# A mixture of experts behind two attentions on one core: blocks of tokens fetched in four parts and transposed in squares of 32 on VectorE

## The chip, the cores and the metric

The kernel runs on one core of a Trainium2 chip. The metric is device time in microseconds for one execution; the kernel before takes 810.36 us (median of 3 runs, 809.91 to 810.59). A core has five engines that matter here: TensorE (PE; its weight loads are listed as PEld), VectorE (DVE), ScalarE (ACT), GpSimd (POOL), and SyncE (SP), which in this kernel only issues DMAs. Each engine works off its own queue in order.

## The reference

2048 tokens (64 sequences of 32) of 256 values pass through cross-attention, self-attention and a mixture of 8 experts, each behind a normalization or on the sum so far. All is in float32. The change touches the experts:

```python
h_NM2H = jnp.einsum('md,ndh->nmh', x_MD, Wl1) + bl1[:, None, :]
a_NMH, b_NMH = (h_NM2H[..., :H], h_NM2H[..., H:])
y_NMD = jnp.einsum('nmh,nhd->nmd', jax.nn.silu(a_NMH) * b_NMH, Wl2) + bl2[:, None, :]
y_MD = jnp.einsum('mn,nmd->md', ew_MN, y_NMD)
```

Here D = 256 and H = 512. `ew_MN` holds the two largest router weights of each token, divided by their sum, and zeros elsewhere. The sum over `d` in the first line is what needs the tokens with their 256 values laid along the partitions.

## The kernel before, in words

**Tokens.** Sixteen tiles of 128 tokens go through cross-attention (64 sequences, `seqs`), self-attention (`self_attention`, L382) and the router (`route`, L470). For each token the router writes a row of `RW` = 265 values (256 normalized values, 8 expert weights, the token's number) to two places of a table in DRAM, `routed`, which has a region of 2048 rows for each expert. These writes are indirect DMAs of POOL (L521), two for each tile of tokens.

**Blocks.** The experts' work is cut into blocks of 128 table rows that belong to one expert. Six "early" blocks are started while the last tokens are still on their way, and 28 "late" blocks follow (up to 33 are provided for; those from 28 on stand in an `If` that isn't entered with these data). A table of where each block begins and whose it is (`meta`) is formed on DVE, for the late blocks in `late_blocks` (L732 to L801), when the last tokens have been counted.

A block takes these steps of the class `Blocks`:

- `gathered` (L608): SP reads the block's first row from `meta` (a TENSOR_LOAD, L586) and issues one DMA of 128 rows x 1060 bytes into the tile xg, one token to a partition. There are five xg buffers.
- `weights` (L614): SP loads the expert's first matrix with its biases (wall1, "W1", 1028 KB) and the second (wall2, "W2", 640 KB) into one of three lanes. A register condition leaves a load out where the lane already holds this expert.
- `prepared` (L624): PE transposes the two halves of xg into a PSUM bank (L629), and ACT copies them to xT (L631), which has two buffers. DVE takes from xg the block's gates and the row numbers to which the results go (L634 to L640).
- `first_half` and `second_half` (L645, L662): PE multiplies xT by the expert's first matrix, eight matmuls each (L657): pa for the gated half, pb for the other. Each shows as two records in the trace. ACT applies silu to pa (L671), DVE multiplies with pb (L676) to g.
- `combined` (L683): PE multiplies g by the second matrix (L688), DVE adds the bias and multiplies by the gate (L693, L694), and POOL adds y to the output by an indirect DMA (L695).

**What sets the order.** The order on SP and PE is the program's (`manual_schedule`, L79); the other engines' order is the planner's, which may bring an instruction forward when its inputs are there. The steps around the last tokens are written out by hand in `do(...)` (L1042 to L1067): x is `prepared`, a and b the halves, c `combined`. The five gathers of the first early blocks are issued at L1017, the sixth at L1058. When `late_blocks` has been called, SP gets the gathers of late blocks 0 to 2 (L1063), then the weights of late block 1 (L1066); late block 0 works with expert 0, whose weights were loaded long before (L1038). Then `run` (L1073) interleaves: in step b it gathers block b + 3, prepares block b + 1, does the first half of b, combines b - 1, loads W2 for b + 2, does the second half of b and loads W1 for b + 3. In the first step `last_early` (L1103) combines the last early block and loads the weights of late block 2.

Of the kernel before, what the change touches and what calls it, by code (L numbers as in the profile page):

```python
# [9 lines left out]
FP = mybir.dt.float32  # L10
U32 = mybir.dt.uint32
AF = mybir.ActivationFunctionType
ALU = mybir.AluOpType
# [3 lines left out]
P = 128  # L17
D = 256
TOK = 2048
NT = TOK // P  # L20
SEQ = 32
# [8 lines left out]
NE = 8  # L30
HID = 512
CAP = TOK
RW = D + NE + 1
# [17 lines left out]
def block_kernel(  # L51
# [23 lines left out]
    nc = tc.nc  # L75
# [4 lines left out]
    const = ctx.enter_context(tc.tile_pool(name="const", bufs=1))  # L80
# [3 lines left out]
    ident = const.tile([P, P], FP, name="ident")  # L84
# [22 lines left out]
    def pool(name, bufs):  # L107
        return ctx.enter_context(tc.tile_pool(name=name, bufs=bufs))
# [19 lines left out]
    for i in range(4):  # L128
        w = slice(4 * HD * i, 4 * HD * (i + 1))
# [29 lines left out]
    routed = tc.dram_tile([NE * CAP, RW], FP, name="routed")  # L159
# [5 lines left out]
    xp = pool("xp", 3)  # L165
    tb = pool("tb", 1)

    def bank(shape, name):
        return ps.tile([P] + shape, FP, tag="a", name=name)
# [415 lines left out]
    def number(meta, k, b, most):  # L585
        return nc.values_load(  # L586
            meta[0:1, k, b : b + 1],
            engines=[SP],
            min_val=0,
            max_val=most,  # L590
            skip_runtime_bounds_check_because="formed from counts that bound it",
        )

    class Blocks:
# [11 lines left out]
            self.xgs, self.xTs, self.ps, self.gs, self.experts = {}, {}, {}, {}, {}  # L606

        def gathered(self, b):  # L608
            xg = xp.tile([P, RW], FP, tag="xg", bufs=5, name=f"xg_{self.name}{b}")
            at = number(self.meta, 0, b, NE * CAP - P)  # L610
            nc.sync.dma_start(out=xg, in_=routed[bass.ds(at, P), :])
            self.xgs[b] = xg

        def weights(self, b, layers, sure=False):  # L614
            if b not in self.experts:
# [7 lines left out]

        def prepared(self, b):  # L624

            xg = self.xgs.pop(b)
            pt = bank([2, P], f"pxT_{self.name}{b}")
            for k in range(2):
                nc.tensor.transpose(pt[:, k, :], xg[:, k * P : (k + 1) * P], ident)  # L629
            xT = xp.tile([P, 2, P], FP, tag="bxT", bufs=2, name=f"bxT_{self.name}{b}")  # L630
            nc.scalar.copy(xT, pt)  # L631
            self.xTs[b] = xT
            gates = xp.tile([P, NE], FP, tag="gates", name=f"gates_{self.name}{b}")
            nc.vector.tensor_tensor(gates, xg[:, D : D + NE], self.mine[:, b, :], ALU.mult)  # L634
            one = slice(b, b + 1)
            nc.vector.tensor_reduce(self.gate[:, one], gates, AX.X, ALU.add)
            if self.valid is None:
                nc.vector.tensor_copy(self.to[:, one], xg[:, RW - 1 : RW])
            else:
                nc.vector.scalar_tensor_tensor(  # L640
                    self.to[:, one], xg[:, RW - 1 : RW], self.valid[:, one],
                    self.spare[:, one], ALU.mult, ALU.add,
                )

# [7 lines left out]
        def of_half(self, b, half):  # L652
            w, _ = lanes[self.lane(b)]
            for j in range(4):
                for k in range(2):
                    lo = k * 2 * HID + (half * 4 + j) * P
                    nc.tensor.matmul(  # L657
                        self.ps[b][half][:, j, :], w[:, lo : lo + P], self.xTs[b][:, k, :],
                        start=(k == 0), stop=(k == 1),
                    )  # L660

# [275 lines left out]

    seen = const.tile([P, NE], FP, name="seen")
    nc.gpsimd.memset(seen, 0.0)
    none = xp.tile([P, RW], FP, tag="xg", bufs=5, name="none")  # L940
    nc.gpsimd.memset(none, 0.0)

    for e in range(NE):
# [231 lines left out]
```

## Time and profile before

| what | value |
|---|---|
| median of 3 runs | 810.36 us |
| the profiled execution's own time | 811.05 us |
| its span, first to last instruction | 809.3 us |
| PE busy | 778.6 us (96%) |
| DVE busy | 496.9 us (61%) |
| ACT busy | 378.3 us (47%) |
| first early gather is issued | 579.34 us |
| first late gather is issued | 638.97 us |
| last late block's last y is added by POOL from | 800.53 us |

Times of instructions are counted from the span's start. In a timeline, each line has the start, the duration, the engine, the line of the kernel, the operation, what is written and read, and how many instructions were merged; brackets hold the idle time of the engine before it and what ended it. "SPq" is SP's queue: the time is that of the issue, not of the transfer. A matmul's duration includes the way through the array, so successive ones overlap, and what a group costs is read from the starts of its neighbours. In a view of windows the columns are the window, its length, the busy time of PE, PEld, DVE, ACT and POOL, the granted clock of PE (1.00 is full), the mean busy share of the 16 DMA engines, and GB/s.

The trace also holds a record for each DMA packet with its start, size and duration. In the late blocks, a gather's packets are 1060 bytes long, those of W1 8224 and those of W2 5120.

### The profile page before, as it was taken

The page shows a single profiled execution, that of the slowest core. Times are in us where ns is not written, and L with a number is a line of the kernel's source. Part 1 is how long each engine was busy: PE and PEld are TensorE (multiplying, and loading weights), DVE is VectorE, ACT ScalarE, POOL GpSimd, SP SyncE. Part 2 cuts the span into 40 slices and gives each one's busy share as a digit, 9 for nine tenths or more (in the row PEclk, how much of TensorE's full clock was granted, in tenths as well). Part 3 has the DMA queues.
Part 4 walks back from the last instruction along what each step waited for, and adds up shares of the span by engine and source line. Part 5 has one row for each costly group of instructions (what it writes and reads, how often), then busy time and mean ns, then how long its engine had stood idle before and what let it go on. Part 6 is the DMA issues. An engine that isn't in the chain of part 4 may idle for free. (4 is left out here: it accounts for less than half of the span.)

```text
span 809.3 us, 15134 instructions
## 1 busy us (share of the span) xinstructions
PE 778.6 (96%) x5212; PEld 612.5 (76%) x5212; DVE 496.9 (61%) x2045; ACT 378.3 (47%) x1078; POOL 143.7 (18%) x195
## 2 busy tenths in 40 slices
PE   8899999999999999999999999999998999999994
PEld 7576777677767767777767777676677899999994
DVE  4657666766686677677677766768665734334332
ACT  3564555556465555556554555555435322222220
POOL 3001011120201011111101110121123313333332
PEclk9999999999999999999999999999999999999998
DMA  9440202021020202022020102020441495356321
GB/s 306 140 112 1 66 11 67 11 89 51 27 79 11 67 10 80 10 75 65 27 66 11 66 11 67 14 73 15 163 162 34 114 398 144 54 139 210 60 41 21
DMA packets 32735, 64.14 MB, mean 79 GB/s; under 512 B 5328, under 2 KB 23632, under 8 KB 31120
## 3 DMA queue, kind: packets, MB, share of 16 engines
q1 hardware_dynamic: 26128, 54.08, 19.8%
q0 software_dynamic: 6528, 9.06, 6.2%
q8 instruction: 43, 0.70, 0.4%
q14 instruction: 36, 0.29, 0.1%
HBM read 87.54 MB, written 13.16 MB: 124 GB/s over the span
## 5 line engine op out<-in xcount | busy, mean ns | idle before, releaser
L314 ACT ACTIVATE pr<-s,nmx 128x257 f32<-128x257 f32 x256 | 121.7, 479 | 110.1 <-DVE nmx L313 101.9
L313 DVE TENSOR_REDUCE nmx<-s 128x1 f32<-128x257 f32 x256 | 105.8, 421 | 70.3 <-PE s L309 69.7
L309 PE MATMUL s<-kv,q 128*128 128x257 f32 x512 | 142.8, 387 | 1.6 <-ACT pr L314 1.4
L342 PE MATMUL pa<-pt,kv 128*128 128x512 f32 x256 | 123.3, 604 | 5.3 <-ACT ov L366 5.3
L309 PEld LDWEIGHTS s<-kv,q 128*128 128x128 f32 x512 | 89.1, 192 | 16.1 <-ACT pt L336 3.0
L332 PEld LDWEIGHTS tp<-ident,pr 128*128 128x128 f32 x512 | 61.5, 144 | 30.4 <-issue 15.7
L321 DVE TENSOR_SCALAR pr<-pr,inv 128x256 f32<-128x256 f32 x256 | 82.3, 363 | 3.3
L521 POOL DMA_INDIRECT routed<-xr,rslots x32 | 32.9, 1027 | 283.6 <-DVE lastT L1006 215.9
L332 PE MATMUL tp<-ident,pr 128*128 128x128 f32 x512 | 80.2, 278 | 1.6 <-DVE pr L321 1.6
L345 ACT COPY cT<-pa 128x512 f32<-128x512 f32 x64 | 37.5, 585 | 89.3 <-PE pa L342 89.3
L336 ACT COPY pt<-tp 128x512 f32<-128x512 f32 x128 | 75.4, 590 | 6.3 <-PE tp L332 6.0
L342 PEld LDWEIGHTS pa<-pt,kv 128*128 128x128 f32 x256 | 46.1, 190 | 39.8 <-issue 28.3
L695 POOL DMA_INDIRECT out_x<-y_late,to_late x28 | 43.5, 1555 | 107.3 <-DMA out_x<-y_late,to_late 33.5
L285 PE MATMUL pqh<-xqT,xwq_sb 128*128 128x256 f32 x256 | 60.8, 381 | 0.8 <-ACT xqT L192 0.8
L375 PE MATMUL po<-xwo_sb,ov 128*128 128x256 f32 x256 | 60.3, 379 | 0.0
L375 PEld LDWEIGHTS po<-xwo_sb,ov 128*128 128x128 f32 x256 | 48.6, 190 | 6.6
L285 PEld LDWEIGHTS pqh<-xqT,xwq_sb 128*128 128x128 f32 x256 | 47.4, 190 | 7.9 <-ACT xqT L192 1.5
L314 ACT ACTIVATION_READ_ACCUMULATOR pr<-s,nmx 128x1 f32 x256 | 51.7, 202 | 0.0
L319 DVE RECIPROCAL inv<-sums 128x2 f32<-128x2 f32 x128 | 20.5, 160 | 44.3 <-ACT pr L314 44.0
L631 ACT COPY bxT_late<-pxT_late 128x256 f32<-128x256 f32 x28 | 10.4, 372 | 73.1 <-PE pxT_late L629 73.1
L390 PE MATMUL pqkv<-awqkv_sb,xaT 128*128 128x512 f32 (+1 forms) x128 | 43.9, 486 | 0.0
L350 POOL TENSOR_TENSOR xb<-x,xbo_bc 128x256 f32<-128x256 f32 x16 | 11.6, 726 | 165.8 <-issue 117.2
(259 smaller groups left out, 1284.0 us busy)
## 6 DMA issues: line engine op xcount, KB each, us to landing
lane<-in_wall SPq DMA_DIRECT2D x24, 1028.0 KB
lane<-in_wall SPq DMA_DIRECT2D x24, 640.0 KB
lane2a<-in_wall SPq DMA_DIRECT2D x10, 1028.0 KB
kv<-in_ctx_t SPq DMA_DIRECT2D x16, 514.0 KB
kv<-in_ctx_a SPq DMA_DIRECT2D x16, 512.0 KB
lane2b<-in_wall SPq DMA_DIRECT2D x10, 640.0 KB
xg_late<-routed SPq DMA_DIRECT2D x28, 132.5 KB
x<-in_x SPq DMA_DIRECT2D x16, 128.0 KB
```

The lines of the kernel that those rows point to most:

```text
L285: nc.tensor.matmul(pq[:, mm, :], xwq_sb[:, k, m * P : (m + 1) * P], xqT[:, k, :], start=(k == 0), stop=(k == 1),)
L309: nc.tensor.matmul(s, qb[:, g * P : (g + 1) * P], kvT[:, b, :], start=True, stop=True)
L313: nc.vector.tensor_reduce(nmx, s, AX.X, ALU.max, negate=True)
L314: nc.scalar.activation(pr[:, g, :], s, AF.Exp, bias=nmx, accum_out=sums[:, g : g + 1])
L321: nc.vector.tensor_scalar(pr[:, i, :ML], pr[:, i, :ML], inv[:, i : i + 1], None, ALU.mult)
L332: nc.tensor.transpose(tp[:, g * P : (g + 1) * P], pr[:, g, j * P : (j + 1) * P], ident)
L336: nc.scalar.copy(pt, tp)
L342: nc.tensor.matmul(pa, kvA[:, b, j, :], pts[j], start=(j == 0), stop=(j == MC - 1))
L345: nc.scalar.copy(cT[:, :, b, :], pa.rearrange("p (h n) -> p h n", n=SEQ))
L375: nc.tensor.matmul(po, ov[:, m, :], xwo_sb[:, m, :], start=False, stop=(m == XH // 2 - 1))
L390: nc.tensor.matmul(pq, xaT[:, k, :], awqkv_sb[:, k, lo:hi], start=(k == 0), stop=(k == 1))
L695: nc.gpsimd.indirect_dma_start(out=out[:, :], out_offset=bass.IndirectOffsetOnAxis(ap=self.to[:, b : b + 1], axis=0), in_=y, in_offset=Non ...
```

## The change

The block's rows are fetched in five DMAs. Four of them bring 64 of the 256 values each, to a quarter of the partitions: partition 32a + i of xg then holds values 64a to 64a + 63 of tokens i, 32 + i, 64 + i and 96 + i. The fifth brings the last nine values of each row (weights and number) to a new tile xw, one token to a partition. One DVE instruction transposes all squares of 32 x 32 of xg into xT, so that partition 32a + i of xT holds values 64a + i and 64a + 32 + i of the 128 tokens. The two PE transposes, the PSUM bank and the ACT copy go. Since this orders the 256 values differently over the partitions, the rows of the first matrix are laid out in the same order on the host. The matmul of L657 then reads its moving operand as four runs of 32 values, 64 values apart, and writes to PSUM contiguously as before. The tile of zeros that clears the table has a place of its own and no longer one of the xg buffers.

```diff
         def gathered(self, b):
-            xg = xp.tile([P, RW], FP, tag="xg", bufs=5, name=f"xg_{self.name}{b}")
+            xg = xp.tile([P, 4, 2 * SEQ], FP, tag="xg", bufs=5, name=f"xg_{self.name}{b}")
+            xw = xp.tile([P, RW - D], FP, tag="xw", bufs=5, name=f"xw_{self.name}{b}")
             at = number(self.meta, 0, b, NE * CAP - P)
-            nc.sync.dma_start(out=xg, in_=routed[bass.ds(at, P), :])
-            self.xgs[b] = xg
+            rows = routed[bass.ds(at, P), :]
+            for a in range(4):
+                nc.sync.dma_start(
+                    out=xg[a * SEQ : (a + 1) * SEQ, :, :],
+                    in_=rows[:, a * 2 * SEQ : (a + 1) * 2 * SEQ].rearrange(
+                        "(c i) e -> i c e", i=SEQ
+                    ),
+                )
+            nc.sync.dma_start(out=xw, in_=rows[:, D:])
+            self.xgs[b] = xg, xw
...
         def prepared(self, b):
-            xg = self.xgs.pop(b)
-            pt = bank([2, P], f"pxT_{self.name}{b}")
-            for k in range(2):
-                nc.tensor.transpose(pt[:, k, :], xg[:, k * P : (k + 1) * P], ident)
-            xT = xp.tile([P, 2, P], FP, tag="bxT", bufs=2, name=f"bxT_{self.name}{b}")
-            nc.scalar.copy(xT, pt)
+            xg, xw = self.xgs.pop(b)
+            xT = xp.tile([P, 4, 2, SEQ], FP, tag="bxT", bufs=2, name=f"bxT_{self.name}{b}")
+            nc.vector.transpose(
+                xT.rearrange("p c k i -> p (c k i)"), xg.rearrange("p c e -> p (c e)")
+            )
             self.xTs[b] = xT
...
-            nc.vector.tensor_tensor(gates, xg[:, D : D + NE], self.mine[:, b, :], ALU.mult)
+            nc.vector.tensor_tensor(gates, xw[:, :NE], self.mine[:, b, :], ALU.mult)
...
                     nc.tensor.matmul(
-                        self.ps[b][half][:, j, :], w[:, lo : lo + P], self.xTs[b][:, k, :],
+                        self.ps[b][half][:, j, :].rearrange("p (c i) -> p c i", c=4),
+                        w[:, lo : lo + P],
+                        self.xTs[b][:, :, k, :],
                         start=(k == 0), stop=(k == 1),
                     )
...
-    none = xp.tile([P, RW], FP, tag="xg", bufs=5, name="none")
+    none = const.tile([P, RW], FP, name="none")
...
+    wl1 = a["L0_ffn_Wl1"].reshape(NE, 4, 2, SEQ, 2 * HID)
+    wl1 = wl1.transpose(0, 1, 3, 2, 4).reshape(NE * P, 2 * 2 * HID)
...
-        "wall1": np.concatenate([by_row("Wl1", 2), by_row("bl1", 8)], axis=1),
+        "wall1": np.concatenate([wl1, by_row("bl1", 8)], axis=1),
```

More of the change, by code (lines that the diff above doesn't have):

```diff
@@ L637, in prepared @@
             if self.valid is None:
-                nc.vector.tensor_copy(self.to[:, one], xg[:, RW - 1 : RW])
+                nc.vector.tensor_copy(self.to[:, one], xw[:, NE:])
             else:
                 nc.vector.scalar_tensor_tensor(
-                    self.to[:, one], xg[:, RW - 1 : RW], self.valid[:, one],
+                    self.to[:, one], xw[:, NE:], self.valid[:, one],
                     self.spare[:, one], ALU.mult, ALU.add,
```

## The prediction

> **What bounds the kernel now.** I read the page first, for the busy shares and the slices.
>
> ```profile
> PE 778.6 (96%) x5212; PEld 612.5 (76%) x5212; DVE 496.9 (61%) x2045; ACT 378.3 (47%) x1078; POOL 143.7 (18%) x195
> ...
> PEclk9999999999999999999999999999999999999998
> DMA  9440202021020202022020102020441495356321
> ```
>
> TensorE is the bound, at full clock, so an instruction taken from it should count. Each slice is 20.2 us: the digits 9 and 5 behind the 14 of the DMA row are 627 to 667 us, where the late blocks begin. Next the timeline of PE in the last blocks, which prices the removed transposes.
>
> ```profile
> 783.82 1.95 PE L657 MATMUL pb_late<-bxT_late,lane 128*128 128x128 f32 x16
> 785.60 0.38 PE L629 MATMUL pxT_late<-ident,xg_late 128*128 128x128 f32 x2
> 785.82 1.95 PE L657 MATMUL pa_late<-bxT_late,lane 128*128 128x128 f32 x16
> ...
> 789.34 1.95 PE L657 MATMUL pb_late<-bxT_late,lane 128*128 128x128 f32 x16
> 791.12 1.06 PE L657 MATMUL pa_late<-bxT_late,lane2a 128*128 128x128 f32 x8
> ```
>
> From start of pb to start of the next pa it is 785.82 - 783.82 = 2.00 us with the two transposes and 791.12 - 789.34 = 1.78 us for the last block, which has none. So a pair costs **0.22 us** of TensorE, not the 0.38 of its row (its matmuls overlap). A block takes 5.52 us, all of it PE. Last, where the late blocks start: PE's timeline, then SP's.
>
> ```profile
> 642.10 0.41 PE L629 MATMUL pxT_late<-ident,xg_late 128*128 128x128 f32 x2 [0.59 <-DMA xg_late<-routed]
> 642.35 1.95 PE L657 MATMUL pa_late<-bxT_late,lane2a 128*128 128x128 f32 x16
> ...
> 645.86 1.95 PE L657 MATMUL pb_late<-bxT_late,lane2a 128*128 128x128 f32 x16
> 647.64 0.38 PE L629 MATMUL pxT_late<-ident,xg_late 128*128 128x128 f32 x2
> ```
>
> ```profile
> 638.97 2.02 SPq L611 DMA_DIRECT2D xg_late<-routed  x3
> 642.03 1.07 SPq L620 DMA_DIRECT2D lane<-in_wall  x2
> 643.63 0.33 SPq L611 DMA_DIRECT2D xg_late<-routed  x1
> 645.02 1.83 SPq L620 DMA_DIRECT2D lane<-in_wall  x2
> ```
>
> SP's order is written by hand: three gathers, then late block 1's weights (W1 and W2), gather 3, block 2's weights. In the trace's DMA packet records block 1's W1 runs from 642.98 to 647.05 us; its pa starts at 647.86. The first gather's last packet ends at 640.65 and PE uses it at 641.07, so 0.42 us pass between packet and use, and W1's **slack is 647.86 - 647.05 - 0.42 = 0.4 us**. This is the tightest place the change touches.
>
> **Removed.** 34 pairs of transposes (6 early, 28 late) x 0.22 = 7.5 us of PE, and 34 ACT copies of 0.37 us that lie beside PE. Only those behind the place that sets the time count: late blocks 3 to 27, 25 x 0.22 = **-5.5 us**. The pairs of late blocks 0 and 1 stand in PE's wait for the gathers, that of block 2 is ahead of block 1's pa, and the early six are ahead of a point set by SP.
>
> **Added on VectorE.** The [128 x 256] transpose isn't in the trace. L1006 (32 columns) takes 203 ns, L445 (128 columns) 302: 1.03 ns a column, so an estimate of 0.43 us at 256; from below 0.30 (L445 itself), from above 1.2 (four times L445, if the partitions went in turn). I take 0.43. In a late block DVE is busy some 2.7 of 5.5 us, and after a block's gates (end at 704.48) it idles 2.28 us before y: the transpose fits there, with 3.5 us to spare before its pa; at 1.2 us it still fits. Without this cover it would cost its 0.43 a block, 12 us. The early part is tighter: DVE is full from 630.6 to 638.4 (the late blocks' table), which ends at SP's release, and an early transpose falling there delays all that follows. From 0 to two of them (0.9), less one 0.22 pair on PE ahead of it: **+0.3**.
>
> **Moving operand in four runs of 32.** No PE row has it. ACT writes 16 runs of 32 values at L345 in 585 ns against 587 contiguous at L336, and DVE reads runs of 16 at L404 in 281 ns against 292 at L441: I take 0, from below 0 as well (a run is 128 contiguous bytes). From above: with 32 such records a block, 0.22/32 = 7 ns on each 111 ns record undoes the whole gain; that is a rival.
>
> **DMAs: the step that decides.** A gather is one issue now; it becomes five, with a register move each, on SP. The nearest row for a short transfer to a part of the partitions is u<-u_last, four issues in 1.83 us, 0.46 apart; with the 0.03 MOVE, **0.50 us each**. From below 0.23 (the shortest gather issue, 0.19, plus its gaps), from above 0.60 (u_last<-u_all, 0.57). Ahead of W1 of late block 1 stand three gathers: 12 x 0.50 = **6.0 us** (2.8 to 7.2). Its issue moves from 642.03 to about 648.0, its packets (3.1 us when alone in the queue, as the later W1 ones; 4.1 here) end near 652.5, and pa of block 1 starts at about 653 and not 647.86. Less the slack 0.4 and some 0.3 of the faster transfer: **+5.3 us**. PE waits from the end of block 0 (about 647.9: its pa starts 0.2 later, since the fourth quarter is issued 1.5 us after the first, and no second pair stands ahead) to 653.
>
> Behind that, W1 of blocks 2 to 6 follow in a full queue. A gather of 128 packets of 1060 B at 48 ns keeps 16 engines for 0.38 us; 512 of 256 B (18 ns for last_sb's) and 128 of 36 B (9 ns) take 0.65, from above 0.95 (27 ns, as xwk_sb's 512 B). So a cycle of loads goes from the 5.0 us of W1's ends to 5.25-5.5, against a PE block of 5.30: from 0 to five blocks x 0.2, **+0.4**. SP also waits for the transfer eight issues earlier:
>
> ```profile
> SPq L96 <- DMA xwo_sb<-in_xwo: 2.2, 1, 2.2
> ```
>
> xwo_sb is load 15, and this gap of SP lies ahead of load 23 (wr_sb, 17.79). Seven issues a block instead of three bring the limit within 1.1 blocks, but a W1 or W2 is always still under way by then, so 0.
>
> The Trainium skill (DMA: Bandwidth & Descriptors, Rules for kernel authors) speaks against the change: one 128-partition transfer instead of several to disjoint partitions, since they share the same engines, and transfers under 64 KB are mostly overhead. By it the loss would lie on the engines, and these quarters are 32 KB; by the packet records the engines lose 0.27 us a gather and SP's issue 2.0. By the rule's reason alone the sum would be near -5, by the rows it is the one below.
>
> **Clock.** In the windows view PE's clock fell once within the work:
>
> ```profile
> 22.00:24.00 2.00, 0.78 (x4) 0.44 (x4) 1.10 (x4) 1.13 (x4) 0.00 (x0) 1.00 0.33 105
> 24.00:26.00 2.00, 1.65 (x5) 1.34 (x6) 0.88 (x5) 0.58 (x1) 0.00 (x0) 0.68 0.84 278
> 26.00:28.00 2.00, 2.00 (x8) 1.65 (x7) 0.72 (x2) 1.38 (x5) 0.00 (x0) 0.50 0.86 174
> ```
>
> After 1.57 us of idle PE it was granted half for 3.4 us (24.7 to 28.1). A wait of 5 us is longer: half clock for 3.4 us loses 1.7. From below 0; I take **+1.7**. The Trainium skill (TensorE: Matmul & The Clock Gate, Part 1) has the clock halved after an idle window of about 3.4 us: by it a 5 us wait may or may not hold a whole window, so 0 or 1.7.
>
> **Sum.** -5.5 + 0.3 + 5.3 + 0.4 + 1.7 = +2.2 us on the profiled 811.05 us (span 809.3 and 1.75 around it): 813.2; against the median 810.36, 0.7 below that execution, **812.6 us**. 0.2% (1.6 us) is about what a measurement of this kernel tells from no change.
>
> **Rivals.**
> 1. *As forecast, without the clock's drop, or with issues of 0.40 us (12 x 0.10 = 1.2 less):* +0.5 to +1.0, about 811. For it: PE's 1.43 us of waiting at 622.2 left the clock at 1.00.
> 2. *Faster: W1 arrives in time.* If a further issue of the same base address costs 0.23 us, W1 is late by 2.8 - 0.7 = 2.1: no drop, -5.5 + 0.3 + 2.1 = -3.1, 807.3; with all else hidden down to -5.5, 804.9. The place is W1 of late block 1; it decides below some 0.35 us an issue, where the lateness is under 3.5. Against it: 0.33 to 0.35 for nearly every gather of now.
> 3. *Slower by more: VectorE waits in the early part.* The five early gathers end at 583 now; with 20 x 0.50 more the fifth lands near 594. DVE takes the gates of these blocks at 586.6 to 589.5, in order, ahead of ov, x and the norms of the last tokens; transposes and gates put at the same place wait for the data, and up to 4 us reach PE (trs at 599.63) and the table behind. Also the first scatter at 588.78 writes the table that these gathers read and would wait to about 594; the second (595.13) and POOL's pow at 596.79 follow it. +2.2 + 4 = +6, 816.6.
> 4. *The transposes come off, but the runs of 32 slow each matmul by 7 ns or more:* no gain, +2.2 + 5.5, 818 or above.
>
> **Chances.** The forecast (+1 to +4) 0.40, of which 0.08 lies within 0.2%; rival 1 0.25 (0.17 within, 0.05 faster, 0.03 slower); rival 2 0.15, faster; rival 3 0.15 and rival 4 0.05, slower. Together faster 0.20, same 0.25, slower 0.55. The range 807.0 to 818.0 leaves out the lower half of rival 2 and the tops of 3 and 4. The forecast alone: 811.3 to 814.4.
>
> **What would show it.** pb to pa 1.78 us in every late block, no L629 and L631 rows; a STREAM_TRANSPOSE of about 0.43 us x34; three gathers from the first issue to W1 in 9 us instead of 3.06; PE idle some 5 us ahead of pa of late block 1, released by a DMA of lane, and 3.4 us at half clock behind. Wrong if W1 is issued before 645.5, if L657 is over 111 ns a record, or if the first late gather moves by more than 1 us from 638.97.

## The result, and the profile after

The changed kernel takes **822.96 us** (median of 5 runs, 820.45 to 824.49), the kernel before 809.91 in the same comparison: a ratio of 1.0155, 95% interval 1.0139 to 1.0172, so 13 us slower. The direction was forecast, the size was not: 812.6 with a range up to 818.0. The profiled execution of the changed kernel took 821.01 us (span 819.1).

The page of the changed kernel, with the rows that were shown of before:

```profile
PE 776.5 (95%) x5144; PEld 609.7 (74%) x5144; DVE 507.7 (62%) x2079; ACT 363.8 (44%) x1042; POOL 143.8 (18%) x195
...
PEclk9999999999999999999999999999998999999998
DMA  9520202101020111102020210200451398448432
```

PE lost 68 instructions, the 34 pairs of transposes, yet its busy time fell by 2.1 us only: 34 x 0.22 = 7.5 went with the transposes, and most of that came back as matmuls at half clock. The 8 in the clock's row is slice 31, 614 to 635 us, well ahead of the late blocks. The last blocks of PE's timeline, and VectorE's group of the new transposes (count, then busy and mean ns):

```profile
714.33 1.95 PE L668 MATMUL pb_late<-bxT_late,lane 128*128 128x128 f32 x16
716.12 1.95 PE L668 MATMUL pa_late<-bxT_late,lane 128*128 128x128 f32 x16
```

```profile
L640 DVE STREAM_TRANSPOSE bxT_late<-xg_late 128x256 f32<-128x256 f32 x28 | 12.2, 436 | 5.6 <-DMA xg_late<-routed 5.6
```

From pb to pa 1.79 us where it was 2.00, and 0.436 us a transpose: both steps of the prediction came out. Then the place that was to decide, late blocks 0 and 1, on SP and on PE:

```profile
644.75 1.88 SPq L616 DMA_DIRECT2D xg_late<-routed  x4
646.82 0.35 SPq L622 DMA_DIRECT2D xw_late<-routed  x1
...
654.00 1.09 SPq L631 DMA_DIRECT2D lane<-in_wall  x2
```

```profile
648.70 2.74 PE L668 MATMUL pa_late<-bxT_late,lane2a 128*128 128x128 f32 x16 [2.10 <-issue]
651.23 2.88 PE L701 MATMUL py_early<-lane,g_early 128*128 128x256 f32 x8
653.95 1.95 PE L668 MATMUL pb_late<-bxT_late,lane2a 128*128 128x128 f32 x16
659.28 3.05 PE L668 MATMUL pa_late<-bxT_late,lane 128*128 128x128 f32 x16 [3.38 <-DMA lane<-in_wall]
662.12 2.56 PE L701 MATMUL py_late<-lane2b,g_late 128*128 128x256 f32 x8
```

W1 is issued 9.25 us behind the first late gather (654.00 - 644.75; it was 3.06), PE waits 3.38 us for it, and pa and py behind the wait take 3.05 and 2.56 us where they took 1.95 and 1.89. All this was forecast. What was not: the first late gather itself is 5.78 us later (644.75 against 638.97). The loss begins in the early blocks, where SP, POOL and PE show how:

```profile
595.49 1.71 SPq L631 DMA_DIRECT2D lane<-in_wall  x2
613.44 1.88 SPq L616 DMA_DIRECT2D xg_early<-routed  x4
...
617.01 2.38 SPq L631 DMA_DIRECT2D lane<-in_wall  x3
```

```profile
605.71 1.67 POOL L708 DMA_INDIRECT out_x<-y_early,to_early  x1 [5.36 <-DMA lane<-in_wall]
607.69 1.01 POOL L521 DMA_INDIRECT routed<-xr,rslots  x1 [0.30 <-issue]
610.55 0.96 POOL L521 DMA_INDIRECT routed<-xr,rslots  x1 [1.86 <-DMA routed<-xr,rslots]
613.44 0.19 POOL L472 COPY xr<-token 128x1 f32<-128x1 f32 x1 [1.93 <-DMA routed<-xr,rslots]
```

```profile
605.28 3.67 PE L668 MATMUL pa_early<-bxT_early,lane 128*128 128x128 f32 x16 [1.62 <-DMA lane<-in_wall]
...
617.13 3.78 PE L668 MATMUL pa_early<-bxT_early,lane 128*128 128x128 f32 x16 [5.37 <-DMA lane<-in_wall]
```

The five early gathers now occupy SP until 593 (583 before), so the weights of early block 1 are issued at 595.49 and not 584.66. The two scatters of tile 13 (counted from 0) into the table have to wait for the gathers that read it; POOL's order now has them behind the first add into out, at 607.69 and 610.55 (588.78 and 595.13 before). The sixth gather, which needs those scatters, is issued at 613.44 (597.88), and behind it on SP stand the weights of early block 2, at 617.01 (601.16). PE waits 1.62 us for the first of these loads and 5.37 us for the second, and both pa take 3.7 to 3.8 us rather than 2.0.

The second of these waits is not for data. SP's rows of the weights in this stretch (count, then shortest, median and longest issue in ns):

```profile
L631 SPq DMA_DIRECT2D lane<-in_wall x8: 73/76/103, 617.0 to 638.9; - x8
```

A load of weights that moves data takes SP 330 ns and more. These eight take 73 to 103, and no packet of 8224 or 5120 bytes starts between 607 and 654 us: the register condition leaves all of them out, since the lanes already hold these experts. PE waits until SP has passed the load that is left out, and pa starts 0.12 us after that.

One thing has to be taken out of the comparison: this execution had no half clock at its start, which cost the profiled execution of before about 2.6 us (its last L380 starts at 595.3, that of after at 592.7). The window that the prediction shows with a clock of 0.68 reads 1.00 here:

```profile
24.00:26.00 2.00, 2.00 (x13) 1.60 (x12) 1.21 (x4) 1.69 (x6) 0.00 (x0) 1.00 0.81 274
```

So the early part really lost 5.78 + 2.6 = 8.4 us.

### The profile page after: what moved, and what is told of

Read it like the earlier page. It is cut to its first block, busy times and chain, and to the rows that moved or that the text cites. A ratio compares the mean times of both kernels' runs of the same rounds, so it can differ in the third digit from the quotient of the medians.

```text
span 819.1 us, 15437 instructions
## 1 busy us (share of the span) xinstructions
PE 776.5 (95%) x5144; PEld 609.7 (74%) x5144; DVE 507.7 (62%) x2079; ACT 363.8 (44%) x1042; POOL 143.8 (18%) x195
## 5 line engine op out<-in xcount | busy, mean ns | idle before, releaser
L684 ACT ACTIVATE sa_late<-pa_late,lane 128x128 f32<-128x128 f32 x72 | 20.6, 369 | 81.2 <-PE pa_late L668 68.7
```

## The experiments

Theory A, in the expectations: the five issues on SP make weights late (8 us in the early part, 6 in the late one, and what the waits bring with them), less the saving on PE. Theory B: the DMAs are hidden, and VectorE or the matmuls in runs of 32 lose the time. Later expectations name their own rival, and theory C where it comes up. Each run's ratio is to the kernel before on the same chip, whose median was 809.1 to 810.7 in these comparisons.

| run | median, us | lowest to highest | ratio, 95% interval |
|---|---|---|---|
| five_dmas | 818.04 | 817.26 to 822.82 | 1.0074 to 1.0116 |
| one_dma | 806.56 | 803.80 to 814.36 | 0.9941 to 0.9993 |
| late_only | 814.31 | 812.76 to 817.69 | 1.0029 to 1.0075 |
| early_only | 819.62 | 819.10 to 820.68 | 1.0095 to 1.0141 |
| sixth_later | 814.28 | 813.90 to 816.30 | 1.0036 to 1.0077 |
| weights_ahead | 814.86 | 813.50 to 815.68 | 1.0038 to 1.0082 |
| late_w1_first | 815.49 | 813.45 to 815.95 | 1.0050 to 1.0089 |
| late_w_first | 815.56 | 814.18 to 816.46 | 1.0058 to 1.0098 |
| late_on_act | 815.30 | 813.49 to 816.40 | 1.0053 to 1.0095 |
| late_filled | 812.42 | 810.82 to 817.65 | 1.0027 to 1.0068 |
| from_3 | 809.17 | 805.32 to 810.91 | 0.9963 to 0.9999 |
| from_8 | 806.50 | 804.76 to 814.02 | 0.9954 to 0.9992 |
| late_one_dma | 810.02 | 806.47 to 813.97 | 0.9974 to 1.0017 |
| late_issues | 814.38 | 814.05 to 816.14 | 1.0037 to 1.0072 |
| late_packets | 807.85 | 805.13 to 810.70 | 0.9957 to 0.9988 |
| late_one_few | 802.22 | 801.99 to 802.73 | 0.9890 to 0.9931 |
| before_few | 808.91 | 807.49 to 810.38 | 0.9982 to 1.0006 |
| after_few | 821.33 | 819.55 to 822.33 | 1.0129 to 1.0174 |

### The two halves of the change: five_dmas and one_dma

five_dmas is the kernel before with its gather cut by columns, still transposed on PE:

```diff
-            nc.sync.dma_start(out=xg, in_=routed[bass.ds(at, P), :])
+            for a in range(4):
+                part = slice(a * 2 * SEQ, (a + 1) * 2 * SEQ)
+                nc.sync.dma_start(out=xg[:, part], in_=rows[:, part])
+            nc.sync.dma_start(out=xg[:, D:], in_=rows[:, D:])
```

> The kernel before, with each gather split into five DMAs (four of 64 values a row, one of 9; all 128 partitions each) and the transposes left on TensorE. Theory A (the five issues on SP are the whole loss: early part some 8 us, 12 further issues ahead of late block 1's weights some 6, the full queue and the clock some 4): the loss without the gain of 5.5, so 809.9 + 18 = 828 us, with the first late gather near 645 and W1 of late block 1 issued 9 us behind it. Theory B (the DMAs are hidden, and VectorE or the runs of 32 lose the time): within 3 us of the kernel before.

one_dma is the changed kernel with one DMA per gather:

```diff
-            for a in range(4):
-                nc.sync.dma_start(out=xg[a * SEQ : (a + 1) * SEQ, :, :], ...)
-            nc.sync.dma_start(out=xw, in_=rows[:, D:])
+            nc.sync.dma_start(out=xg, in_=rows)
```

> The changed kernel, with one DMA a gather as before; the rows lie one token to a partition, so the squares that VectorE transposes aren't those of the reference and the experts' products are of mixed values: the same instructions on the same shapes, another result. Theory A: the gain without the loss, 5.5 to 7.5 us faster than before, 802.5 to 804.5 us; pb to pa 1.78 us, no wait of PE at late block 1. Theory B: slower than before, 815 or more.

The issues alone lose some 8 us, and VectorE's half alone loses nothing: theory B falls. But neither number is theory A's. In five_dmas POOL kept tile 13's scatters ahead of the add into out (598.54 and 605.23), the sixth gather came at 609.25, and the early part lost less than in the changed kernel: its first late gather is issued at 642.14, 3.2 us later than in the kernel before. (This is the profile of its slowest run, 822.82 us, which also had the half clock at its start.) So the 24 early issues alone account for some 3 us, and the other 5 came with POOL's order. And one_dma gains 2.7 us (0.9967) where some 7 were due, with runs from 803.8 to 814.4. What such a spread can come from, the last runs show.

### The two places: late_only and early_only

The new way for the blocks of one class alone, the other as before, with both orders of W1 in memory.

> The six early blocks by the old way (one DMA, two TensorE transposes), the 28 late ones by the new; the first matrix is there in both orders. Theory A: the early part's 8 us are gone, the late part's +6 -0.5 +4 -5.5 stay: +2 to +4, 812 to 814 us, first late gather at 636 to 639. Theory B: near the changed kernel, since 28 of 34 blocks are as in it: 820 or more.

> The six early blocks by the new way, the late ones by the old. Theory A: the early part's loss alone, +7 to +9, 817 to 819 us; PE waits some 5 us ahead of pa of early block 2, which is released as its weights' DMA passes on SP behind the sixth gather. Theory B: 6 of 34 blocks of the loss, +2, 812.

Early +9.2 us, late +3.9 us, together the 13. The early blocks, which the prediction had at +0.3, make two thirds of the loss. In late_only the first late gather is not delayed (636.34), and its W1 follows at 646.03, 9.7 us behind.

### The early part: sixth_later and weights_ahead

```diff
     do("near far x0")
-    blocks.gathered(EARLY - 1)
     do("far near near a0 far x1 b0 near far near near c0 near a1 near far b1 x2 far a2 near c1")
+    blocks.gathered(EARLY - 1)
```

> The changed kernel with one edit: the five issues of the sixth early gather stand on SP behind the weights of early blocks 2 and 3, no longer ahead of them. Theory A (the weights that stand on SP behind the gathers are late): the wait of 5.4 us ahead of pa of early block 2 goes, and what it brought the clock: 816 to 819 us. Theory B (the early part loses its time to the gathers' own transfers, or to VectorE, whatever the order on SP): 821 to 824 us, as the changed kernel's 822.96.

This one edit to the changed kernel took 8.7 us off by the medians (7.9 by the ratios), more than expected. POOL's order stayed the changed kernel's (scatters at 607.38 and 611.30), so it is the place of the sixth gather on SP that costs. SP, with the weights of early blocks 1 to 3 in one run of six issues, ahead of the sixth gather:

```profile
596.15 19.12 SPq L631 DMA_DIRECT2D lane<-in_wall  x6
615.83 2.27 SPq L616 DMA_DIRECT2D xg_early<-routed  x4
```

The wait of 5.37 us is gone; 1.1 us for the weights of early block 1 is left. weights_ahead puts gathers 2 to 5 behind those weights as well:

```diff
             blocks.weights(0, (0, 1), sure=True)
-            for i in range(EARLY - 1):
-                blocks.gathered(i)
+            blocks.gathered(0)
...
     blocks.weights(1, (0, 1), sure=True)
+    for i in range(1, EARLY - 1):
+        blocks.gathered(i)
```

> As the run before, and the early gathers 2 to 5 stand behind the weights of early block 1 as well. Theory A: no early weights are late any more, so only the late part's loss is left, that of the run with the change in the late blocks alone (814.3 us): 812 to 816. Theory B: 820 to 824. In between, 816 to 820, if the scatter of tile 14, which comes later still, puts a wait in the place of the one that goes.

It is within what theory A gave, and no further gain. PE now runs ahead and stands 6.89 us before late block 0, whose gather is issued at 638.42. The table of late blocks is ready at 633.3 already; SP's waits in this stretch (total, count, longest) show what holds that gather:

```profile
SPq L616 <- DMA routed<-xr,rslots: 4.6, 1, 4.6
```

It is the last scatter into the table, which POOL starts at 635.59. In sixth_later it is the same (4.8 us); in late_only that scatter is started at 631.64, and the gather goes when the table is ready. So the order on SP makes 8.7 of the early part's 9.2 us by the medians, but on PE a part of the loss is left. From the start of PE's last pov matmuls (L358 of the kernel before, near 585 us, ahead of all that differs) to the end of its last block it takes 223.87 us in the changed kernel, 218.21 in weights_ahead and 216.10 in late_only. The medians hide these 2.1 us, because late_only ends 2.7 us behind its last y, with the chain of adds that is described below.

### The late part: which order, which engine

late_w1_first is late_only with W1 of late block 1 ahead of the gathers of blocks 1 and 2; late_w_first also puts the gathers of blocks 2 and 3 behind the weights of block 2; late_on_act issues the gathers of late blocks 1 and above from ScalarE.

```diff
     do("c3")
-    for b in range(3):
-        late.gathered(b)
-    do("b4 x5 a5 c4")
-    late.weights(1, (0, 1))
+    late.gathered(0)
+    do("b4 x5 a5")
+    late.weights(1, (0,))
+    late.gathered(1)
+    do("c4")
+    late.weights(1, (1,))
+    late.gathered(2)
     do("b5")
```

> The change in the late blocks alone (814.31 us before this edit), with W1 of late block 1 put ahead of the gathers of late blocks 1 and 2 on SP, and W2 ahead of that of block 2. Theory A (twelve issues ahead of that W1): the first W1 is issued some 3 us behind the first late gather rather than 9.7, the wait of 5 to 6 us and the half clock behind it go, and the 25 pairs of transposes are saved: 804.5 to 807.5 us, below the kernel before (810.4). Theory B (the DMA queue is full there, and whatever comes first delays the rest): a wait of the same size appears ahead of pa or pb of late block 1 or 2, 811 to 815 us.

> As late_w1_first (815.49 us, where the wait of 3.7 us had moved to W1 of late block 2, issued at 652.4 behind the gathers of blocks 2 and 3), with these two gathers behind the weights of late block 2. Theory A (the issues on SP, in which order they stand): both W1 in time, only the wait ahead of late block 0 and its half clock stay: 806 to 809.5 us. Rival (the DMA queue is full there, and any order makes something late): a wait ahead of late block 2, 3 or 4 takes its place, 811 to 816.

> The change in the late blocks alone, with the gathers of late blocks 1 and above issued from ScalarE, that of block 0 still from SP. Theory A (SP's time for the issues makes W1 late): 5 issues rather than 17 are ahead of W1 of late block 1, and SP has two or less per block behind it, so no W1 is late; the wait of 2.3 us ahead of pa of late block 0 and the half clock behind it stay: 806 to 809 us. Rival (the transfers themselves, whoever issues them, or ScalarE's own work is held up): 811 us or above.

All three missed theory A's number; none is below late_only. With W1 of block 1 in time, PE waits 1.2 us for the rows of block 1 and 3.7 us for W1 of block 2 (issued at 652.44); with that in time too, 3.3 us for the rows of block 2 and 2.6 for the W1 of block 4. From ScalarE, W1 of block 1 is issued 3.5 us behind the first gather and PE has no wait there, but ScalarE's sa of late block 0 stands 13.5 us behind its gathers, and py, g and later weights wait in turn. Between 640 and 665 us something always is last in the list; the order only chooses what.

### Issues or packets: late_one_dma, late_issues, late_packets

These three tell SP's time from the DMA queue's. The first is late_only with one DMA per gather. The other two add one thing each:

```diff
+            for a in range(4):
+                part = slice(2 * a, 2 * a + 2)
+                nc.sync.dma_start(out=xw[0:1, part], in_=rows[0:1, part])
```

```diff
+            parts = rows[:, : 4 * (2 * SEQ + 1)].rearrange("p (c e) -> p c e", c=4)
+            nc.sync.dma_start(out=xg, in_=parts[:, :, : 2 * SEQ])
+            nc.sync.dma_start(out=xw, in_=rows[:, D:])
```

> The late blocks alone, transposed in squares on VectorE, but each gathered by one DMA as before (the rows are not put in quarters, so the product mixes columns of four rows; times only). The ground line for the next two. Both theories: W1 is issued 3 us behind the first late gather, nothing is added to the DMA queue, 28 pairs of transposes of 0.22 us are saved: 803 to 806 us. 808 or above would mean that the squares on VectorE cost time themselves.

> The run before, and four further DMAs per late gather on SP that move 8 bytes each: the number of issues of the change, none of its bytes or packets. Theory A (SP's time for the issues): W1 of late block 1 is issued 9 us behind the first late gather again and the waits of the change in the late blocks alone (814.31 us) are back, less that ahead of late block 0, whose rows come with the first issue: 809 to 815. Theory B (the queue's time for the small packets, 0.44 us of all 16 engines for each gather by the page's shares, (175.3 - 160.2) / 34): 803 to 806.5.

> Two DMAs per late gather: one that brings the row in four pieces of 64 values each (every piece ends one value short of the next, so that each is a packet of its own; the values are shifted and not put in quarters, times only), and one for the gates. The packets of the change without its issues. Theory A: 3 further issues of 0.5 us ahead of W1 of late block 1, not 12: 804 to 808. Theory B: the queue is as full as with the change: W1s late by 2 us and more, 810 to 815.

By the medians, four DMAs of 8 bytes bring back the whole time of late_only (814.38 against 814.31). PE's timeline of late_issues:

```profile
644.07 1.95 PE L685 MATMUL pb_late<-bxT_late,lane2a 128*128 128x128 f32 x16
652.19 3.75 PE L685 MATMUL pa_late<-bxT_late,lane 128*128 128x128 f32 x16 [6.17 <-DMA lane<-in_wall1s]
655.74 3.02 PE L715 MATMUL py_late<-lane2b,g_late 128*128 128x256 f32 x8
```

W1 is issued 9.5 us behind the first gather (646.48 - 636.99). The packets without most of the issues cost a wait of 2.3 us, and the run stays below before. The medians of these runs end with the chain of adds, so PE alone is the cleaner measure. From the start of the last pov matmuls to the end of PE's last block it takes 211.57 us in the kernel before, 206.00 in late_one_dma, 209.59 in late_packets, 215.42 in late_issues and 216.10 in late_only. The squares save 5.6 us, the four small issues cost 9.4, the packets with one further issue 3.6, and the whole change 10.1. So SP's issues are the main cause in the late part. The Trainium skill (DMA: Bandwidth & Descriptors, Rules for kernel authors) advises one transfer over 128 partitions for the reason that disjoint ones share the same engines; the advice holds here, but the loss lay on the issuing side. The same section says that spreading issues over engines saves sequencer time only; late_on_act shows that the time saved on SP was then missing on ScalarE.

The ground line was the surprise: 810.02 us, where 803 to 806 were due, with only 1.63 us of waiting on PE in the late blocks.

### The chain of adds: late_one_few, before_few, after_few

PE's last block in late_one_dma ends at 791.88, seven us before the kernel before's (799.07; 5.6 us from the same pov matmuls on), and the last y is ready at 792.73. POOL's timeline shows what happens then, first in late_one_dma, then in the kernel before:

```profile
792.24 1.55 POOL L718 DMA_INDIRECT out_x<-y_late,to_late  x1 [3.07 <-DMA out_x<-y_late,to_late]
796.86 1.55 POOL L718 DMA_INDIRECT out_x<-y_late,to_late  x1 [3.07 <-DMA out_x<-y_late,to_late]
801.40 1.55 POOL L718 DMA_INDIRECT out_x<-y_late,to_late  x1 [2.99 <-DMA out_x<-y_late,to_late]
```

```profile
790.63 1.55 POOL L695 DMA_INDIRECT out_x<-y_late,to_late  x1 [3.96 <-DVE y_late L694]
795.93 1.55 POOL L695 DMA_INDIRECT out_x<-y_late,to_late  x1 [3.75 <-DVE y_late L694]
800.53 1.55 POOL L695 DMA_INDIRECT out_x<-y_late,to_late  x1 [3.05 <-DVEq L1117]
```

Each add into out waits for the one before. They follow each other by 4.4 to 4.6 us at best, and in the kernel before by 8.7 to 9.6 us between 641 and 669 us, where the weights of the first late blocks are under way. So the chain falls behind there, and afterwards gains 5.52 - 4.55, about 1 us a block, on PE. It falls behind once more between 723 and 742 us (5.6 to 6.9 us an add), where the only later loads of W1 lie: by the packets nine loads move data in the late blocks, six from 643 and three from 722 us. In the kernel before the chain has caught up by 780 us: its adds wait for y. With the transposes gone a block takes 5.30, the catching up is slower, and the last add of late_one_dma starts 8.7 us after its y. To test it, the adds of late blocks 2, 5, 8 to 26 were left out:

```diff
+            if self.name == "late" and b % 3 == 2 and b < 27:
+                return
             nc.gpsimd.indirect_dma_start(
```

> The run late_one_dma (810.02 us, 806.5 to 814.0) with the scatter-adds into out of late blocks 2, 5, 8 and so on to 26 left out (their tokens lack that share). Theory C (the adds are a chain of their own: each waits for the one before it, 4.5 us a block at least and 8 to 10 while the weights are moved, so it ends behind TensorE, 8.7 us late in that run's profile): the end follows TensorE's, whose last block ended at 791.9, so 802 to 804.5 us, and the runs lie close together. Rival (the spread and the missing gain come from the clock, as 0.990 to 0.994 in these runs): 806 to 814 as before.

> The kernel before with the same adds left out. Theory C: there the chain has just caught up with TensorE (the last add starts 0.6 us after its y is ready), so 0 to 1 us less: 808.5 to 810.5 us. Were the chain the bound already: 806 or below.

> The changed kernel with the same adds left out. Theory C: TensorE's last block is so late (808.9) that the chain hardly matters (last add 0.7 us after its y): 820 to 823 us. If the chain were what makes the changed kernel slow: 815 or below.

All three came as theory C had them: late_one_few at 802.22 us with runs 0.7 us apart, the kernel before unchanged (0.9994, 0.9982 to 1.0006), the changed kernel nearly so (1.0152 against 1.0155). The chain is no part of the 13 us; it is why a change that speeds up PE gains little here even without the issues.

### The clock, and the versions that win: late_filled, from_3, from_8

late_filled is late_only with matmuls that nobody reads in PE's two waits:

```diff
+            if self.name == "late" and b < 2:
+                pf = bank([P], f"pf{b}")
+                for _ in range((7, 13)[b]):
+                    nc.tensor.matmul(pf, ident, ident, start=True, stop=True)
             self.of_half(b, 0)
```

> The change in the late blocks alone (814.31 us), with matmuls that nobody reads (identity by identity, 7 ahead of pa of late block 0 and 13 ahead of pa of late block 1, some 0.27 us each) in TensorE's two waits there, 2.29 and 3.77 us in that run's profile. Theory A (behind those waits pa took 3.66 and 3.75 us rather than 1.95 and py 3.16 rather than 1.89, 4.8 us in all, because the clock falls while TensorE waits): the waits stay, the 4.8 us go, 808.5 to 811 us, so more work makes it faster. Rival (the slow matmuls have another cause than the wait before them, as their layout): 813.5 to 816.

PE's timeline of late_only, then of late_filled:

```profile
640.50 3.66 PE L692 MATMUL pa_late<-bxT_late,lane2a 128*128 128x128 f32 x16 [2.29 <-DVE gates_late L664]
```

```profile
638.94 1.73 PE L683 MATMUL pf<-ident 128*128 128x128 f32 x14
641.19 2.05 PE L696 MATMUL pa_late<-bxT_late,lane2a 128*128 128x128 f32 x16 [0.52 <-DVE bxT_late L653]
```

The pa behind the filled wait takes 2.05 us and not 3.66. That the layout is not the cause is plain from the other late blocks, whose pa in the same layout take 1.95. That filling the wait helped rests on this one execution, and the clock also stayed full behind an unfilled wait of this length in two runs (2.27 us in late_packets, 2.17 in late_on_act). In the profiled execution W1 was later still and the second wait outlasted its filling. The median is 1.9 us lower, with intervals that overlap: for the whole effect the runs are inconclusive.

from_3 and from_8 use the new way from late block 3 or 8 on only; every second column goes to k = 0, so that one order of W1 serves both ways:

```diff
+        def in_squares(self, b):
+            return self.name == "late" and b >= 8
```

> The new way for late blocks 3 and above only, the old one for the early blocks and late blocks 0 to 2; every second column goes to k = 0, so one order of W1 serves both ways. Theory A: the lists on SP that were late are as before, and 22 pairs of transposes of 0.22 us are saved: 804.5 to 807.5 us (kernel before 810.4). Theory B (squares on VectorE or the matmuls in runs of 32 cost more than the transposes): 810 us or above.

> The new way for late blocks 8 and above only (20 of 28), one order of W1, every second column to k = 0. In the run from block 3 on W1 of late block 2 was still 1.9 us late and the clock fell behind it; from block 8 on the weights have room on SP and in the queue. Theory A: no wait is added, 20 pairs of 0.22 us are saved, 4.4 us: 804.3 to 806.5 us (kernel before 809 to 810.4). Rival (the squares cost about what they save wherever they stand): 808.5 us or above.

from_8 is faster than both kernels, than the kernel before by 0.3%: 806.50 us, 0.9973 (0.9954 to 0.9992) of it. Its median is at the upper end of theory A's range. In its profile no weights are late by more than 0.2 us, since between 670 and 719 us no load of W1 moves data; PE's last block ends 3.4 us earlier than in the kernel before, counted from the pov matmuls (208.14 against 211.57), where 20 pairs come to 4.4; its last add starts at 796.35, 2.1 us after its y (794.29). That is the chain again. from_3 still has a wait of 1.87 us for W1 of late block 2 and half clock behind it.

## Why the prediction was wrong, point by point

The forecast was +2.2 us and the result is +13. Slower was right, but the reason that was given for it, the late part, makes only 3.9 us of the 13 (late_only; by its interval 2.3 to 6.1) and was forecast at 1.9. The early part makes 9.2 and was forecast at 0.3.

- **The early blocks, +0.3: the step that failed.** In the sum it priced only the transposes on VectorE. The 24 issues that the six early gathers add on SP stand in it at nothing, and the early six are called "ahead of a point set by SP", while the same issues ahead of W1 of late block 1 were counted with care. Rival 3 did count 20 of them and had the place half right: the fifth gather at 594 (it was 593) and the scatter that waits for it. It led them to PE through VectorE, for 4 us, with a chance of 0.15. They went through the scatters and the sixth gather to the weights of early block 2 behind it on SP, with POOL's order changed as well. The profile has 8.4 us, the runs 9.2 (early_only) and 8.7 (sixth_later). The prediction's own sign of being wrong, a first late gather moved by more than 1 us, is this step.
- **The saving, -5.5: right on PE.** From pb to pa it is 1.79 us, and late_one_dma's PE ends 5.6 us earlier. The prediction took all of PE's time for time of the kernel. The adds' chain stood 0.6 us behind y already, and the runs in which PE alone got faster (late_one_dma against late_one_few) show that most of the saving would have gone there. In the changed kernel itself this doesn't count, since PE ends so late (last add 0.7 us after its y).
- **Twelve issues, +5.3: right.** They took 0.52 us each (9.25 - 3.06 = 6.19 over 12). From the first late gather to pa of block 1 it is 14.53 us, 5.64 more than before (647.86 - 638.97 = 8.89).
- **The full queue, +0.4: too small.** PE waited 1.7 us for the W1 in lane2a further on, at 689.54.
- **The clock, +1.7: right behind late block 1, and missing elsewhere.** There pa and py took 1.10 and 0.67 us longer. The same happened twice in the early part (pa of blocks 1 and 2, 1.7 us each), which is inside the 8.4.
- **A misreading without effect.** The digits 9 and 5 behind the 14 of the DMA row are slices 33 and 34, 647 to 688 us, not 627 to 667. No term rests on it.

The profiled executions add up: 8.4 early, +5.64, and from pa of block 1 to the last add 151.12 us against 152.67, -1.55; together 12.5, less the 2.6 of the start, 9.9. The spans differ by 9.8.

Two things stay open. Why POOL's order put the scatters behind the add in the changed kernel and not in five_dmas was not tried. That the adds take 8 to 10 us because of the weights' transfers is argued from the times alone.

## What to carry to other kernels

Before splitting a DMA, count its new issues on every stretch of the queue that issues it, and look for what stands behind each: the price is paid by the next transfer with a deadline, not by the split one. When an engine at 95% gets work taken away, look for the next chain that runs at nearly the same pace, and measure its backlog over the whole run, not only at the end. Where a transfer must be split, do it where its queue has room: the new way from late block 8 on wins, if only 2.6 us. A load that a condition leaves out still has its place in the queue, and whoever waits for it waits until the queue gets there.

## What the runs showed of the hardware

- A DMA of 8 bytes costs SP nearly as much as one of 32 KB: four of them took 1.57 us in late_issues, four quarters 1.88 in the changed kernel.
- Dependent indirect adds into one tensor followed each other by 4.4 us at the least, mostly 4.5 to 4.6, of which POOL works 1.55.
- A load of weights that its register condition left out took SP 73 to 103 ns and moved no packet, yet PE's pa of early block 2 started only behind it (617.13, after 617.01).
- PE's clock fell to half behind every wait of 3.3 us and more, and behind shorter ones only sometimes: after 1.62 and 2.10 (the changed kernel), 1.87 (from_3) and 2.29 us (late_only), but not after 2.17 (late_on_act), 2.27 (late_packets) or 2.58 (late_w_first). The same wait near 24 us did it in the profile of before (1.57 us) and not in that of after (1.58). The Trainium skill (TensorE: Matmul & The Clock Gate, Part 1) has a free-running window of about 3.4 us; the dependence on more than the wait's length agrees, but here waits well below one window were enough.
- The moving operand in four runs of 32 costs nothing: pb's records take 275 ns before and after.
